# A four-layer graph network on one core: the adjacency check ahead of the last features, a table first in its queue, fp16 keys

## The chip, the core and the metric

The kernel runs on one core of a Trainium2 chip. A core has five engines with instruction queues of their own: PE (TensorE, matrix products; the load of its stationary operand is shown apart as PEld), DVE (VectorE), ACT (ScalarE), POOL (GpSimd) and SP (SyncE, which here only starts transfers). They meet through semaphores. Matrix products land in PSUM, which is handed out in banks of 128 x 512 fp32; all else lies in SBUF. Transfers from and to HBM run on 16 DMA engines, whichever engine starts them. The metric is the device time of one execution, in microseconds (us). A "granted clock" of 1.0 means that PE ran at its full clock.

## The reference, cut to what matters

x is 8 batches x 2048 nodes x 64 features; adj is a 2048 x 2048 matrix of zeros and ones with ones on its diagonal, thinner towards high node numbers; H says which of 64 hyperedges each node belongs to. Four layers follow one another, each `x = x + layer(relu(layernorm(x)))`. The change touches only work that belongs to layer 0:

```python
h = x @ W
maskEN = H.T
s = leaky_relu(h @ a_node, 0.2)
logits = where(maskEN[None, :, :] > 0, s[:, None, :], NEG)
alpha = softmax(logits, axis=-1)                  # per hyperedge, over its nodes
agg = einsum('ben,bnf->bef', alpha, h)
beta = sigmoid((h @ a_gn)[:, None, :] + (agg @ a_ge)[:, :, None])
all_he = elu(beta[..., None] * h[:, None] + (1.0 - beta[..., None]) * agg[:, :, None])
deg = maximum(adj.sum(-1), 1.0)[:, None]
industry = einsum('nm,bmf->bnf', adj / deg, x @ W_ind)
...
```

Behind these lines each node mixes its own hyperedges' `all_he` with softmax weights, and mixes the result with `industry`. Layers 1 to 3 use adj again: a graph convolution, three rounds of messages, and attention over neighbours.

## The kernel before

The kernel does not treat adj and H as dense where it need not. A node's hyperedges and near neighbours are worked through one "place" at a time, over nodes sorted by how many they have. Fixed lists in the program (`HELD`, `TIED`, `LISTED`) say for how many tiles of 128 nodes each place is made. So the kernel starts with a check that adj holds only zeros and ones and that no count exceeds those lists. The check ends in one integer, `flag`, and a branch: with 0 the short way is taken, with 1 the dense one. The branch is taken by every engine for itself, and each reads the flag first; no instruction crosses it.

Node features are kept as four tiles q, each of 128 partitions (two batches x 64 features) by 2048 nodes, worked in four chunks of 512 columns (`CW`). There are 16 tiles of 128 nodes (`NT`). The order of the instructions on each engine is not written out by hand: a scheduler sorts them by the order of the program text and by what is ready in its own estimate, within one side of the branch. What is written earlier gets the earlier turn.

**start (L594)** does three things at once. For each chunk, the layer norm: centering products (`bank<-x_ch,center`), squares, the row sums, then SQRT on ACT, RECIPROCAL on DVE (`std`, L287), the spread of the scale to all rows (`bank<-std,from_rows`), and DVE's product with it (L605). One chunk later, `features` (L649): h as h_t (features by nodes: `bank<-q,ww`, L656) and as h_n (nodes by features: `bank<-ww,q`, L662), both copied out of PSUM by ACT. And `check_adj` (L353): for each of the 16 row blocks of adj, 1 MB is loaded (L371), squared on ACT into `squares` with the row sum as `deg` (L372), and compared with its square on DVE (L373). POOL sets the diagonal to zero (L376) and starts a store to `links` (L380). PE counts the links of each pair of blocks with 13 one-column products (`seen`).

In the text, the check's matter stands behind `features` of the last chunk (L629), and its end behind the PSUM pools of the norm. That end is a row of small operations on DVE: `edges` from `seen` (L387), `count_nodes` (L422) with `classes` (L415), which makes one comparison of 128x16 for each possible count and one 128x1 comparison for each limit (L446), `crowded_lists` (L399) with 15 such comparisons (L408), joins of the maxima (L634), a transpose by PE (L636), and the flag (L639). Beside it 1/deg goes out to `rdeg` (L640 to L646).

**layer0_pairs (L782)** is the arm behind the branch. It loads `fcw` (L681), and then runs three things interleaved by a generator:

- `ranks` (L460): from the hyperedge counts of the nodes, each node's place in the sorted order, by prefix sums on DVE, with `classes` once more.
- `hyperedge_keys` (L564): for each chunk of 512 ranks and each of the 16 node tiles, a one-hot matrix `hot` (L582: is the column number equal to the node's rank?), 64 in all, and its product with H's mask (`twice`, loaded at L570).
- `aggregate` (L880): it stores h_n to `h_rows` in HBM (16 stores, L895), makes the nodes' scores (L904 to L908), loads H transposed into `cap` (L912, two transfers of 512 KB, into the slot that `squares` had), turns it into limits (L913, L914), and then for each q: `logits` (L923), their maximum (L925), the exponentials on ACT (L927), 16 transposes (L934) copied out as `et` (L182, L184), 16 products into `pa`, and some twenty small steps from `agg` to `both`.

Behind them come `by_rank` (L504, the sorted order as gather indices), the preparation of link lists, the product of adj with `x_ind` (L316), and `Pairs` (L2223), whose `fetch` gathers sorted rows of `h_rows` on POOL (L2249). SP's queue is in program order: `fcw`, the 16 stores of h_rows, HT, H, `w_ind`, then adj's blocks.

Of the kernel before, what the change touches and what calls it, by code (L numbers as in the profile page):

```python
# [19 lines left out]
P = 128  # L20
# [114 lines left out]
class Kernel:  # L135
# [76 lines left out]
    def setup(self):  # L212
# [7 lines left out]

        self.center = c.tile([P, P], F, name="center")
# [131 lines left out]
    def check_adj(self, pool, slots, seen):  # L353


        nc, adj = self.nc, self.a["adj"]
        rows = [slots.tile([P, 2, N], F, name=f"rows{i}", tag=f"q{6 + i}") for i in range(2)]
# [29 lines left out]
        nc.vector.tensor_scalar(self.edges, seen, 0.0, None, op0=OP.is_gt)  # L387
        bad = pool.tile([P, 1], F, name="bad")
        nc.vector.tensor_reduce(bad, same, axis=AX.X, op=OP.add)
        nc.vector.tensor_scalar(bad, bad, float(N * NT), None, op0=OP.is_lt)  # L390
# [5 lines left out]
        nc.vector.tensor_sub(own, deg, own)  # L396
        return bad, deg, own

    def crowded_lists(self, pool, ones, ps):  # L399

        nc = self.nc
        pn = ps.tile([P, NT, FAR], F, name="pn")
        self.mm(pn.rearrange("p t i -> p (t i)"), ones, self.edges.rearrange("p t i -> p (t i)"))
        total = pool.tile([P, NT], F, name="listed_total")
        nc.vector.tensor_reduce(total, pn, axis=AX.X, op=OP.add)
        nc.vector.memset(total[:, :1], 0.0)
        for t in range(1, NT):
            nc.vector.tensor_scalar(  # L408
                total[:, t : t + 1], total[:, t : t + 1], float(P * LISTED[t]), None, op0=OP.is_gt
            )  # L410
        bad = pool.tile([P, 1], F, name="listed_bad")
        nc.vector.tensor_reduce(bad, total, axis=AX.X, op=OP.max)
        return bad

    def classes(self, w, deg, J):  # L415

        least = w.tile([P, J + 2, NT], BF, name=f"least{J}")
        for i in range(J + 2):
            self.nc.vector.tensor_scalar(least[:, i], deg, float(J + 1 - i), None, op0=OP.is_ge)
        return least  # L420

    def count_nodes(self, pool, slots, adj_deg):  # L422

        nc = self.nc
        hm = slots.tile([P, NT, D], F, name="hm", tag="q9")
        nc.sync.dma_start(hm, self.a["H"].rearrange("(t p) e -> p t e", p=P))
        nc.vector.tensor_scalar(hm, hm, 0.0, None, op0=OP.is_gt)
        deg = self.deg
        nc.vector.tensor_reduce(deg[:, 0], hm, axis=AX.X, op=OP.add)
        nc.vector.tensor_copy(deg[:, 1], adj_deg)  # L430
        ones = pool.tile([P, P], BF, name="ones")
        nc.vector.memset(ones, 1.0)
        for which, held in enumerate((HELD + [0], TIED)):
            J = len(held) - 1
            least = self.classes(pool, deg[:, which], J)
            with self.tc.tile_pool(reuse_waits="tile", name="count_ps", bufs=1, space=PSUM) as ps:
                pn = ps.tile([P, (J + 2) * NT], F, name="pn")
                self.mm(pn, ones, least.rearrange("p k t -> p (k t)"))
                total = pool.tile([P, J + 2], F, name=f"total{which}")
                nc.vector.tensor_reduce(  # L440
                    total, pn.rearrange("p (k t) -> p k t", t=NT), axis=AX.X, op=OP.add
                )
            over = pool.tile([P, J + 2], F, name=f"over{which}")
            nc.vector.memset(over, 0.0)
            for i in range(J + 1):
                nc.vector.tensor_scalar(  # L446
                    over[:, i : i + 1], total[:, i : i + 1], float(P * held[J - i]), None,
                    op0=OP.is_gt,
                )
            if which == 0:  # L450
                nc.vector.tensor_scalar(
                    over[:, J + 1 :], total[:, J : J + 1], float(N), None, op0=OP.is_lt
                )
            bad = pool.tile([P, 1], F, name=f"crowded{which}")
            nc.vector.tensor_reduce(bad, over, axis=AX.X, op=OP.max)
            yield bad
        with self.tc.tile_pool(reuse_waits="tile", name="listed_ps", bufs=1, space=PSUM) as ps:
            yield self.crowded_lists(pool, ones, ps)
# [105 lines left out]
    def hyperedge_keys(self, w, bank, both, rank, key):  # L564
# [5 lines left out]
        nc.sync.dma_start(got, self.a["H"].rearrange("(t p) e -> p t e", p=P))  # L570
# [4 lines left out]
        line, _ = self.numbers(w, CW)  # L575
# [18 lines left out]
    def start(self, pool, slots):  # L594
# [4 lines left out]
        self.self_weight = pool.tile([P, NT], F, name="self_weight")  # L599
        with tc.tile_pool(reuse_waits="tile", name="k00", bufs=1) as k:  # L600
# [6 lines left out]
            with (  # L607
                tc.tile_pool(reuse_waits="tile", name="links_ps", bufs=1, space=PSUM) as lps,
                tc.tile_pool(reuse_waits="tile", name="ln", bufs=2) as w,
                tc.tile_pool(reuse_waits="tile", name="ln_ps", bufs=7, space=PSUM) as ps,  # L610
# [10 lines left out]
                for ch in range(NC):  # L621
# [5 lines left out]
                    if ch > 0:  # L627
                        self.features(ww, ch - 1, bank)
# [3 lines left out]
            with tc.tile_pool(reuse_waits="tile", name="check_ps", bufs=1, space=PSUM) as ps:  # L632
                for crowded in self.count_nodes(k, slots, adj_deg):
                    nc.vector.tensor_max(bad, bad, crowded)  # L634
# [245 lines left out]
    def aggregate(self, slots, raw, h_t, h_n, fcw, av, both, agg_hi, agg_lo):  # L880
        nc, tc, a = self.nc, self.tc, self.a
        with (
# [11 lines left out]
            for t in range(NT):  # L894
                nc.sync.dma_start(self.h_rows[t * P : (t + 1) * P, : NB * D], h_n(t))  # L895
# [2234 lines left out]
```

## Time and profile before

| what | us |
|---|---|
| runs, median of 3 | 2026.12 |
| runs, lowest to highest | 2022.63 to 2032.97 |
| profiled execution, whole | 1975.97 |
| profiled execution, span | 1974.2 |
| PE busy / DVE busy / POOL busy / ACT busy | 1699.7 / 1408.2 / 1035.1 / 809.4 |
| flag written (end of L639) | 106.43 |
| first gather of h_rows (L2249) | 211.20 |

The page cuts the span into 40 slices of 49 us. Busy shares are in tenths; PEclk is the granted clock in tenths; the first five slices hold all the work that the change touches:

```profile
PE   6859889999997887999999999778989899579885
...
DVE  6778778884677674877677656588989676459774
...
PEclk8868899998996888999999989889989999689887
DMA  9740223345335776233131111277788774666665
```

The 16 row blocks of adj pass in the first two slices, with the DMA engines nearly full; in the fourth slice (148 to 197 us) they stand still. A group row of the profile reads: line, engine, operation, output<-input, shapes, count, then busy us, mean ns of one, and the idle time just ahead of it with what ended most of it. In a timeline row the first number is the start, the second the time that the row covers; "x8" means eight instructions merged, and a matrix product in fp32 counts as two. Brackets hold the idle time before it. "SPq" rows are the starting of transfers, not the transfers themselves.

### The profile page before, as it was taken

Reading aid. Unit: us, or ns where it says so; the run is one execution under the profiler, and the core shown is the slowest. Engines: PE = TensorE matmul, PEld = TensorE weight load, DVE = VectorE, ACT = ScalarE, POOL = GpSimd, SP = SyncE. Lnnn points to the kernel's source line nnn. Section 1 sums busy time; section 2 is a strip of 40 time slices with the busy share of each in tenths; the row PEclk is TensorE's granted clock in tenths of the full one; section 3 lists DMA queues with packets and bytes.
Section 4 is the critical chain, followed back from the end, with each engine's and each line's share of the span. In section 5 each row is a group of like instructions: output and inputs, shape, how many; then the busy total and the mean of one; then the engine's idle time right before and its main releaser. Section 6 shows DMA issues by size and latency. Waiting matters only on the chain. (4 is left out here: it accounts for less than half of the span.)

```text
span 1974.2 us, 22337 instructions
## 1 busy us (share of the span) xinstructions
PE 1699.7 (86%) x7066; PEld 971.8 (49%) x7066; DVE 1408.2 (71%) x2389; ACT 809.4 (41%) x1627; POOL 1035.1 (52%) x959
## 2 busy tenths in 40 slices
PE   6859889999997887999999999778989899579885
PEld 2515666665324454444443444356767566345432
DVE  6778778884677674877677656588989676459774
ACT  5712344454664663222111010255666664267300
POOL 1100166766870743876765635266375641478771
PEclk8868899998996888999999989889989999689887
DMA  9740223345335776233131111277788774666665
GB/s 345 263 120 1 77 75 102 109 128 178 99 101 174 239 218 188 78 87 117 47 99 53 48 67 41 96 223 234 246 257 286 222 259 164 228 186 172 183 177 195
DMA packets 124057, 305.20 MB, mean 155 GB/s; under 512 B 29312, under 2 KB 31120, under 8 KB 118160
## 3 DMA queue, kind: packets, MB, share of 16 engines
q0 software_dynamic: 45328, 149.60, 25.2%
q1 hardware_dynamic: 76288, 149.80, 22.5%
q10 hardware_dynamic: 2304, 4.20, 0.6%
q8 instruction: 59, 0.97, 0.2%
q14 instruction: 78, 0.64, 0.1%
HBM read 240.40 MB, written 63.14 MB: 154 GB/s over the span
## 5 line engine op out<-in xcount | busy, mean ns | idle before, releaser
L2578 POOL DMA_INDIRECT raw<-sent,index x300 | 313.8, 1046 | 308.3 <-DVE part_lo L2596 156.3
L2596 DVE TENSOR_TENSOR part_lo<-raw,part_hi 128x512 fp32r<-128x512 f32 x352 | 266.2, 777 | 119.3 <-ACT part_hi L2595 108.8
L2595 ACT CAST part_hi<-raw 128x512 fp32r<-128x512 f32 x352 | 212.5, 619 | 319.0 <-PE acc L176 211.6
L1840 POOL TENSOR_TENSOR half<-half,y 128x512 f32<-128x512 f32 x192 | 247.3, 1318 | 134.0 <-DVE y L1834 128.8
L176 PE MATMUL pk<-q,w 128*128 128x512 f32 (+1 forms) x768 | 301.6, 610 | 2.4 <-DVE q L1724 0.9
L176 PE MATMUL acc<-q,ident 128*128 128x512 f32 x416 | 202.3, 613 | 22.7 <-DVE q L2909 16.5
L176 PE MATMUL acc<-part_hi,weights 128*128 128x512 f32 x365 | 177.0, 488 | 27.3 <-ACT part_hi L2595 26.7
L1834 DVE SCALAR_TENSOR_TENSOR y<-pk,bias,q 128x512 f32<-128x512 f32 x224 | 158.0, 742 | 52.1 <-PE pk L176 32.9
L176 PEld LDWEIGHTS pk<-q,w 128*128 128x128 f32 (+1 forms) x768 | 115.8, 190 | 156.0 <-issue 120.2
L176 PE MATMUL acc<-part_lo,weights 128*128 128x512 f32 x365 | 167.5, 460 | 23.3 <-DVE part_lo L2596 22.7
L2819 POOL DMA_INDIRECT ring<-f_rows,near x121 | 142.8, 1180 | 64.6 <-issue 29.6
L176 PEld LDWEIGHTS acc<-q,ident 128*128 128x128 f32 x416 | 77.1, 194 | 96.4 <-issue 43.6
L2305 POOL TENSOR_TENSOR q<-q,beta 128x512 f32<-128x512 f32 x57 | 76.1, 1337 | 72.4 <-DVE beta L2281 33.8
L176 PEld LDWEIGHTS acc<-part_hi,weights 128*128 128x128 f32 x365 | 73.7, 202 | 79.4 <-ACT part_hi L2595 45.8
L176 PEld LDWEIGHTS acc<-part_lo,weights 128*128 128x128 f32 x365 | 73.9, 202 | 73.5 <-DVE part_lo L2596 57.8
L176 PE MATMUL pp<-adj,x_ind_hi 128*128 128x512 f32 x256 | 89.3, 464 | 0.5 <-DVE q L846 0.3
L2564 ACT CAST hub_weights<-dense 128x384 fp32r<-128x384 bf16 x80 | 40.6, 511 | 102.6 <-PE acc L176 98.2
L2890 DVE TENSOR_TENSOR q<-ring,e 128x1024 f32<-128x1024 f32 x58 | 70.0, 1218 | 8.7 <-PE acc L176 8.5
L2305 POOL TENSOR_TENSOR q<-q,coef 128x512 f32<-128x512 f32 x57 | 63.1, 1108 | 20.9 <-DVE q L2328 17.6
L176 PE MATMUL pp<-adj,x_ind_lo 128*128 128x512 f32 x256 | 72.7, 403 | 0.0
L287 DVE RECIPROCAL std<-std 128x512 f32<-128x512 f32 x16 | 53.6, 3351 | 25.5 <-ACT std L286 21.6
L2489 POOL DMA_INDIRECT listed_raw<-in_adjT_dram,cell x60 | 62.2, 1037 | 16.5 <-issue 15.9
(503 smaller groups left out, 3421.6 us busy)
## 6 DMA issues: line engine op xcount, KB each, us to landing
rows<-in_adj_dram SPq DMA_DIRECT2D x16, 1024.0 KB, 9.2
adj_t<-in_adjT_dram SPq DMA_DIRECT2D x64, 256.0 KB, 3.0
own<-sent SPq DMA_DIRECT2D x52, 256.0 KB, 4.3
raw<-sent SPq DMA_DIRECT2D x52, 256.0 KB, 3.5
sent<-u SPq DMA_DIRECT2D x48, 256.0 KB, 3.7
q<-x SPq DMA_DIRECT2D x10, 1024.0 KB, 5.1
x<-q SPq DMA_DIRECT2D x9, 1024.0 KB, 4.0
links<-squares POOLq DMA_DIRECT2D x16, 512.0 KB, 8.2
```

The costliest lines, as they stand in the source:

```text
L176: self.nc.tensor.matmul(out, lhsT, rhs, start=start, stop=stop)
L287: nc.vector.reciprocal(std, std)
L1834: nc.vector.scalar_tensor_tensor(y, pks[b, half], bias[:, b : b + 1], emb[:, b], op0=OP.add, op1=OP.mult,)
L1840: add.tensor_add(acc, acc, y)
L2305: self.nc.gpsimd.tensor_tensor(x, x, by.unsqueeze(2).to_broadcast([P, NB, D]), op=OP.mult)
L2489: self.kern.behind(nc.gpsimd.indirect_dma_start(raw[:, i], None, rows, bass.IndirectOffsetOnAxis(ap=self.cell[:, c + i : c + i + 1], axis= ...
L2564: self.nc.scalar.copy(to, self.lists.dense[:, :, i * P : (i + 1) * P])
L2578: self.nc.gpsimd.indirect_dma_start(raw, None, self.rows[:], bass.IndirectOffsetOnAxis(ap=self.lists.index[:, c : c + 1], axis=0),)
L2595: nc.scalar.copy(hi, raw)
L2596: nc.vector.tensor_sub(lo, raw, hi.bitcast(F))
L2819: self.nc.gpsimd.indirect_dma_start(to, None, self.kern.f_rows[:], bass.IndirectOffsetOnAxis(ap=index, axis=0))
L2890: nc.vector.tensor_tensor(y.rearrange("n i (b f) -> n i b f", b=NB), block[:, i : i + 2, : NB * D].rearrange("n i (b f) -> n i b f", b=NB) ...
```

## The change

It has five parts.

1. Limits in tables. A constant `falling` (128x22, made by 22 one-column memsets on POOL in `setup`) holds the falling counts, so that `classes` is one DVE comparison of two broadcast operands instead of one operation for each count. `limits` puts all limits into one row, again by memsets on POOL. `count_nodes` and `count_lists` compare whole rows with it, into one tile `over` whose maximum is taken once.
2. `check_adj` holds all of the check up to the flag and 1/deg, and is called ahead of `features` of the last chunk. The hyperedges' counts are taken ahead of adj's. Its small products share one PSUM bank (`chain`) in the pool of `seen`; the norm's pool gets six banks instead of seven.
3. In `aggregate` the loads of HT and of H come first; the 16 stores of h_rows move behind the transposes of `raw`, four with each q.
4. The key's column numbers are fp16 instead of fp32.
5. The column numbers come from their own iota; the row numbers that `numbers` made along with them, and nobody read there, are gone.

```diff
 def setup(self):
+        self.falling = c.tile([P, NEAR[1] + 2], F, name="falling")
+        for i in range(NEAR[1] + 2):
+            nc.gpsimd.memset(self.falling[:, i : i + 1], float(NEAR[1] + 1 - i))
...
-    def check_adj(self, pool, slots, seen):
+    def check_adj(self, pool, slots, seen, ps, flag):
+        limit = self.limits(pool)
+        over = pool.tile([P, limit.shape[1] + 2], F, name="over")
...
-        nc.vector.tensor_scalar(self.edges, seen, 0.0, None, op0=OP.is_gt)
+        hm = slots.tile([P, NT, D], F, name="hm", tag="q9")
+        nc.sync.dma_start(hm, self.a["H"].rearrange("(t p) e -> p t e", p=P))
+        nc.vector.tensor_scalar(hm, hm, 0.0, None, op0=OP.is_gt)
+        nc.vector.tensor_reduce(self.deg[:, 0], hm, axis=AX.X, op=OP.add)
+        self.count_nodes(pool, ones, limit, over, 0, ps)
+        nc.vector.tensor_sub(self.deg[:, 1], deg, own)
+        self.count_nodes(pool, ones, limit, over, 1, ps)
...
+        nc.vector.tensor_scalar(over[:, -2:-1], bad, float(N * NT), None, op0=OP.is_lt)
+        nc.vector.tensor_scalar(self.edges, seen, 0.0, None, op0=OP.is_gt)
+        self.count_lists(pool, ones, limit, over, ps)
+        nc.vector.tensor_reduce(bad, over, axis=AX.X, op=OP.max)
+        pt = ps.tile([P, CW], F, name="chain")[:1, :P]
+        nc.tensor.transpose(pt, bad, self.ident)
+        one = pool.tile([1, 1], F, name="one")
+        nc.vector.tensor_reduce(one, pt, axis=AX.X, op=OP.max)
+        nc.vector.tensor_scalar(flag, one, 0.0, None, op0=OP.is_gt)
...
     def classes(self, w, deg, J):
         least = w.tile([P, J + 2, NT], BF, name=f"least{J}")
-        for i in range(J + 2):
-            self.nc.vector.tensor_scalar(least[:, i], deg, float(J + 1 - i), None, op0=OP.is_ge)
+        full = [P, J + 2, NT]
+        self.nc.vector.tensor_tensor(
+            least, deg.unsqueeze(1).to_broadcast(full),
+            self.falling[:, NEAR[1] - J :].unsqueeze(2).to_broadcast(full), op=OP.is_ge,
+        )
         return least
+    def limits(self, pool):
+        held = [HELD + [0], TIED]
+        values = [P * n for x in held for n in x[::-1]]
+        values += [3e9] + [P * n for n in LISTED[1:]]
+        limit = pool.tile([P, len(values)], F, name="limit")
...
+            self.nc.gpsimd.memset(limit[:, at : at + n], float(values[at]))
...
+    def count_nodes(self, pool, ones, limit, over, which, ps):
+        J = (len(HELD), NEAR[1])[which]
+        at = which * (len(HELD) + 1)
+        least = self.classes(pool, self.deg[:, which], J)
+        pn = ps.tile([P, CW], F, name="chain")[:, : (J + 2) * NT]
+        self.mm(pn, ones, least.rearrange("p k t -> p (k t)"))
+        total = pool.tile([P, J + 2], F, name=f"total{which}")
+        nc.vector.tensor_reduce(
+            total, pn.rearrange("p (k t) -> p k t", t=NT), axis=AX.X, op=OP.add
+        )
+        nc.vector.tensor_tensor(
+            over[:, at : at + J + 1], total[:, : J + 1], limit[:, at : at + J + 1], op=OP.is_gt
+        )
...
 def hyperedge_keys(self, w, bank, both, rank, key):
-        nc.sync.dma_start(got, self.a["H"].rearrange("(t p) e -> p t e", p=P))
...
-        line, _ = self.numbers(w, CW)
+        whole = w.tile([P, CW], I32, name="whole")
+        nc.gpsimd.iota(whole, pattern=[[1, CW]], base=0, channel_multiplier=0)
+        line = w.tile([P, CW], F16, name="line")
+        nc.vector.tensor_copy(line, whole)
...
 def start(self, pool, slots):
-                tc.tile_pool(reuse_waits="tile", name="ln_ps", bufs=7, space=PSUM) as ps,
+                tc.tile_pool(reuse_waits="tile", name="ln_ps", bufs=6, space=PSUM) as ps,
...
+                self.check_adj(k, slots, seen, lps, flag)
                 self.features(ww, NC - 1, bank)
-                bad, deg, adj_deg = self.check_adj(k, slots, seen)
...
 def aggregate(...):
-            for t in range(NT):
-                nc.sync.dma_start(self.h_rows[t * P : (t + 1) * P, : NB * D], h_n(t))
...
+            for s in range(2):
+                nc.sync.dma_start(cap[s * D : (s + 1) * D], a["HT"])
+            load()
             for ch in range(NC):
...
-            for s in range(2):
-                nc.sync.dma_start(cap[s * D : (s + 1) * D], a["HT"])
...
                     nc.tensor.transpose(pt[:, i], raw[:, t * P : (t + 1) * P], self.ident)
+                    nc.sync.dma_start(self.h_rows[t * P : (t + 1) * P, : NB * D], h_n(t))
```

`load` is the load of H that left `hyperedge_keys`.

## The prediction

> **What bounds the kernel now.** I read the page first, then the engines' busy time in short stretches, then the timeline and the waits of the first 212 us, since every edited line runs there. The page's chain of waits names only the tail, so it does not say what the edited stretch is worth. The stretches do. After the time, the columns are PE, PEld, DVE, ACT and POOL busy (with instruction counts), granted clock, DMA share, GB/s:
>
> ```profile
> 97.40:107.10 9.70, 1.56 (x5) 0.30 (x4) 8.20 (x92) 0.00 (x0) 0.00 (x0) 0.68 0.01 2
> 107.10:119.00 11.90, 6.17 (x34) 1.19 (x34) 10.68 (x52) 3.93 (x7) 1.90 (x6) 0.68 0.85 312
> 119.00:128.00 9.00, 2.24 (x4) 0.58 (x4) 1.84 (x6) 1.90 (x3) 0.00 (x0) 0.64 1.07 237
> 128.00:146.50 18.50, 15.20 (x37) 6.31 (x38) 16.96 (x29) 2.68 (x3) 0.32 (x2) 0.53 0.01 3
> 146.50:164.00 17.50, 17.19 (x90) 10.55 (x89) 16.63 (x41) 4.93 (x9) 0.00 (x0) 0.90 0.00 1
> ```
>
> From 97.4 to 107.1 one chain of 92 tiny DVE instructions runs and everything else stands. From 119 to 128 nearly nothing runs, while the DMA engines are full. From 128 to 164 DVE is busy for 92 and 95% of the stretches. The timeline gives the ends of those waits (start, duration, then in brackets the idle time and what ended it):
>
> ```profile
> 89.17 3.60 PE L176 MATMUL bank<-q,ww 128*128 128x512 f32 x8
> 92.60 3.73 PE L176 MATMUL bank<-ww,q 128*128 128x128 f32 x32
> 96.17 1.22 PE L176 MATMUL seen<-one_bf,squares 128*128 128x1 bf16 x43
> ...
> 97.43 0.37 DVE L387 TENSOR_SCALAR edges<-seen 128x208 bf16<-128x208 f32 x1 [6.96 <-PE seen L176]
> ...
> 106.29 0.14 DVE L639 TENSOR_SCALAR flag<-one 1x1 int32<-1x1 f32 x1
> 107.19 0.55 DVE L683 COPY av<-cols 128x128 f32<-128x128 f32 x1 [0.76 <-DVE flag L639]
> ...
> 108.39 10.17 SPq L895 DMA_DIRECT2D h_rows<-q  x16
> 118.81 1.95 SPq L912 DMA_DIRECT2D cap<-in_HT_dram  x2
> 127.98 1.23 DVE L913 TENSOR_SCALAR cap<-cap 128x2048 f32<-128x2048 f32 x1 [7.16 <-DMA cap<-in_HT_dram]
> ```
>
> PE works off 7.3 us of the last chunk's features before the 43 link counts that DVE waits for (6.96 us); then the check's chain takes 9.0 us (97.43 to 106.43); then the arm starts; its table HT is queued behind 16 stores and comes 7.16 us late.
>
> **1. The start, a small loss.** 22 one-column memsets (`falling`) now stand on POOL ahead of the memset of `ww`, and SP's first queue waits for that memset before it loads `ww` and then x. The nearest row is 15 short memsets at L2440, 0.57 us together, of 115 ns each: one starts every (0.57 - 0.115) / 14 = 0.033 us, so 22 x 0.033 = 0.7 us. At present `ww` is ready at 1.15 and its load starts at 1.26, so there is almost no slack, and the first matmul waits for x until 8.04. Take **+0.7**; bounds 0 and 22 x 0.115 = +2.5. The 25 short memsets of `limit` follow the identity on POOL, which is next needed at 19.55: hidden, about 1 us if it weren't.
>
> **2. The check.** Removed from the path: the wait behind the features. The new order on PE puts the link counts ahead of them, and the features fill PE's waits for DVE. On DVE the loops become tables; the rows of 97 to 108 (busy us, mean ns):
>
> ```profile
> L446 DVE TENSOR_SCALAR over<-total 128x1 f32<-128x1 f32 x34 | 2.5, 136 | 0.0
> L419 DVE TENSOR_SCALAR least<-deg 128x16 bf16<-128x16 f32 x22 | 1.9, 163 | 0.0
> L408 DVE TENSOR_SCALAR listed_total<-listed_total 128x1 f32<-128x1 f32 x15 | 1.1, 143 | 0.0
> ```
>
> These 5.5 us become one 128x352 comparison, priced by the 128x208 TENSOR_TENSOR rows (366 ns at L488) at about 0.55, and two of 0.15. There is one maximum instead of three, with no joins.
>
> A wait is added: the first count (`total<-chain`, 128x14) stands on DVE ahead of the last chunk's RECIPROCAL, now at 74.76, and waits for a matmul that stands on PE behind 46 link counts. These start at 73.93 and come every 0.03, so it ends near 75.5, and the 0.38 reduction makes the RECIPROCAL start near 75.9: **+1.1**. Behind it are the scale factors, PE's products with them, and DVE's last two comparisons, so I count it whole (bounds 0 to +1.5). Three small operations between the last comparisons add 0.4.
>
> So the last comparison ends not at 90.06 but at 90.06 + 0.7 + 1.1 + 0.4 = 92.3. Then: last link count 93.0 (one feature product of 0.9 stands before it); product 0.9 and the 128x352 count to 94.4; reduction 0.53, edges' count and reduction to 95.9; limits and maximum to 96.2; one product and a quarter of a tile on PE, transpose, maximum, flag near 97.5; the transpose and copy of `rows`, which stand before the branch on DVE, to 98.4. With the 0.76 of the branch DVE starts the arm at 99.1, and SP with it (its store of `rdeg` waits for that copy, between its reading of the flag and its branch). PE still has 12 x 0.23 = 2.8 us of features, reaches the branch at 100.9 and the arm's first matmul near 101.6; DVE would want it at 99.1 + 1.9 - 0.55 = 100.5, so PE is late next. That matmul was at 109.06. **Net -7.5**, the two losses of 1 and 2 included; bounds -6 (the features hold it) and -9.5 (losses 0, features hidden). PSUM: six banks for seven; of the nine banks that a norm takes, the one reused sixth was read long before, so 0, up to +1.
>
> **3. HT first.** SP issues `fcw` (1.11), HT (1.95), H (0.58) and only then the 16 stores. HT's issue ends 3.1 us into the arm; its 1 MB, with nothing ahead, takes as long as the x loads of 1 MB (5 to 8 us by their rows), so it is there about 9 us in at worst. DVE asks at 99.1 + 9 (the work now from 107.2 to 116.7, less the shorter `least`): no wait left. **-7.2**, bounds -5 and -7.2. H is wanted five us later still. HT's load waits for the last `links` stores out of the same slot: issued at 90.7, 8.2 us to land, so 99 to 101, about when SP gets there. The stores of h_rows move behind; first reader is the gather at 211.20, 100 us later: hidden. The gathers and the mask on POOL change places with some memsets: under 1 us, beside matmuls.
>
> **4. The rank's `least`** in the arm: 13 of 0.073 spacing (0.95) become one of about 0.4: **-0.55**. One 0.15 cast falls away too.
>
> **5. One-hot keys from fp16.** The 64 keys, and the nearest 16-bit row:
>
> ```profile
> L582 DVE TENSOR_SCALAR hot<-linef,rank_here 128x512 bf16<-128x512 f32 x64 | 28.0, 479 | 3.2 <-PE bank L176 3.0
> L2437 DVE TENSOR_SCALAR q<-q,ownf 128x780 bf16<-128x780 bf16 x1 | 0.4, 421 | 0.0
> ```
>
> Keys start 0.395 us apart (six in 2.46 us). The 780-column 16-bit row, 421 ns, is shorter than the 512-column fp32 one: fp32 costs 0.49 ns a column (1227 ns at 2048 less 479 at 512), so 16-bit near half of that, 0.25. 512 x 0.245 = 0.13 us each, 64 x 0.13 = 8.3 us of DVE. How much reaches the end? [...] The trace: granted clock 0.53 at 128 to 146.5 and 0.90, 0.75, 0.92 in the three stretches to 206.5; the same bf16 products come every 0.43 us in the first and every 0.22 when warm; DVE waits on PE for 11 us already (`aggs` 5.6, `hot` 3.0, `et` 2.3). [...] a product at 0.43 is slower than a key at 0.27, PE paces the stage, and the fp16 part gives 0: the total would be -15.2. By the rows the clock does return, and up to 8.3 comes through: -23.6. Between them I take half, by the rows, since two of three stretches were at 0.9: **-4.3**.
>
> **Sum**: -7.5 - 7.2 - 0.55 - 4.3 = **-19.5**. The profiled execution took 1974.2 in its span and 1.8 around it: 1976.0 becomes 1956.5. The median of the runs is 2026.1, 50 us above that execution, with a spread of 10; nothing in the trace tells why. I take off the same microseconds (in proportion it would be 20.0): **2006.6**.
>
> **Rivals.** About 0.5% (10 us) is what can be told from no change.
> A, as above, about 2006 (2001 to 2013): 0.55.
> B, DVE sets the pace throughout: all 8.3 come through[...]: -24 to -30, about 2000: 0.20. For it: DVE 92 to 95% busy at 128 to 164; against: PE busy at 20.5 of 20.5 at 164 to 184.
> C, PE paces the arm and the features hold the branch: -6 - 7.2 - 0.5 = -13.7, about 2012: 0.13.
> D, it doesn't do what it says: HT still comes late behind the `links` stores (say 5 of 7.2 lost) and the check ends behind the features (-4): about 2020: 0.08. Against: 2 GB/s in the stretch before the arm.
> E, slower: granted clock. PE is busy 1541 us after 212 us, at 0.911 on the mean, with slices between 0.6 and 0.9. If the earlier start shifts the later bursts so that the mean falls by 1.3%, to 0.899, 20 us are gone; from 0.893 (30 us) it is slower by 0.5%, about 2037. For it: clock differs among stretches of like work; against: those later stages have the same instructions and waits. 0.04.
> The range 1991 to 2018 leaves out the ends of A and B, most of D, and E, under 0.2 together. Faster 0.83, same 0.13 (D and the edges of A and C), slower 0.04.
>
> **What would show it.** First matmul near 8.7; RECIPROCAL of the last chunk near 76.5; flag near 97.5, arm near 99 to 101; no wait for HT; keys at about 0.35 us of duration; the gather of h_rows near 191.5 instead of 211.2; after that, the same distances between stages. Wrong it would be if that gather comes 20 us earlier and the end doesn't, if a key still takes 0.48, or if the flag comes after 103.

## The result, and the profile after

| | before | after |
|---|---|---|
| median, us | 2026.76 (2022.63 to 2032.97, 4 runs) | 2001.78 (1985.33 to 2011.05, 4 runs) |
| ratio | | 0.9876, 95% interval 0.9835 to 0.9917 |
| the same two on another chip (that of e5 to e8), median, us | 2025.42 (14 runs) | 1998.68 (6 runs) |
| ratio there | | 0.9854, 95% interval 0.9813 to 0.9896 |
| profiled execution, span, us | 1974.2 | 1983.5 |

The kernel is 25 us faster (16.8 to 33.4 by the interval), where 19.5 were forecast. The two profiled spans show the opposite sign: the profile of before lies 50 us below that kernel's own other runs, the one of after only 16. The spans are therefore no measure of the change. On the chip of e9 to e12 below, 44 runs of the kernel before took 1970.24 to 1986.89, median 1979.06, 46 us less than on that of e5 to e8: the level goes with the chip, and the profile of before, 1975.97, fits the faster one. On which chip it was taken is not on record. The stretch that the change touches is a better measure, and it is compared up to the first gather of h_rows.

The timeline of the changed kernel, with the rows that answer to those shown of before (start, duration, in brackets the idle time and what ended it):

```profile
75.70 0.69 ACT L290 ACTIVATE std<-bank,eps 128x512 f32<-128x512 f32 x1 [0.65 <-PE bank L176]
77.08 0.39 DVE L461 TENSOR_REDUCE total<-chain 128x14 f32<-128x224 f32 x1 [2.53 <-PE chain L176]
77.39 3.34 DVE L291 RECIPROCAL std<-std 128x512 f32<-128x512 f32 x1
...
91.37 1.19 PE L176 MATMUL seen<-one_bf,squares 128*128 128x1 bf16 x42
93.60 0.38 DVE L405 TENSOR_SCALAR edges<-seen 128x208 bf16<-128x208 f32 x1 [0.40 <-PE seen L176]
97.22 0.14 DVE L412 TENSOR_SCALAR flag<-one 1x1 int32<-1x1 f32 x1
97.49 2.84 PE L176 MATMUL bank<-ww,q 128*128 128x128 f32 x24
98.42 0.25 DVE L692 COPY av<-cols 128x128 f32<-128x128 f32 x1 [0.46 <-DVE rows L424]
...
100.32 1.10 SPq L917 DMA_DIRECT2D cap<-in_HT_dram  x2
102.16 15.36 SPq L1003 DMA_DIRECT2D h_rows<-q  x16
107.82 1.23 DVE L930 TENSOR_SCALAR cap<-cap 128x2048 f32<-128x2048 f32 x1 [1.31 <-DMA cap<-in_HT_dram]
184.78 0.58 DVE L962 TENSOR_SCALAR aggs<-pa,den 64x64 f32<-64x64 f32 x2 [2.58 <-PE pa L176]
185.61 0.38 SPq L1009 DMA_DIRECT2D h_rows<-hb  x1
189.49 1.02 POOL L2267 DMA_INDIRECT q<-h_rows,order  x1 [1.24 <-DMA h_rows<-hb]
```

And of the kernel before, the rows of these events that were not shown yet:

```profile
74.04 0.69 ACT L286 ACTIVATE std<-bank,eps 128x512 f32<-128x512 f32 x1 [0.65 <-PE bank L176]
74.76 3.35 DVE L287 RECIPROCAL std<-std 128x512 f32<-128x512 f32 x1 [0.84 <-ACT std L286]
...
206.32 0.58 DVE L945 TENSOR_SCALAR aggs<-pa,den 64x64 f32<-64x64 f32 x2 [2.59 <-PE pa L176]
207.15 0.37 SPq L991 DMA_DIRECT2D h_rows<-hb  x1
211.20 1.02 POOL L2249 DMA_INDIRECT q<-h_rows,order  x1 [77.77 <-DVE upto L544]
```

The wait for the link counts fell from 6.96 to 0.40 us; the check's chain runs from 93.60 to 97.36 instead of 97.43 to 106.43, and TensorE works on features beside it. HT's loads start 18.5 us earlier, and the wait for them fell from 7.16 to 1.31. A new wait, 2.53, stands ahead of the RECIPROCAL. The gather comes at 189.49 instead of 211.20.

What the gather waits for is not the sorted order, which is ready some 30 us earlier, but the last write into h_rows, the store of `hb`. That is made of `raw`, the nodes' scores, which in before are complete at 120.3 us, but by its turn in the program it stands right behind the last `aggs`; no run wrote it earlier. In all 14 profiles of this case that store starts 3.9 to 4.6 us ahead of the gather, whatever engine its row names as the releaser. So the arm up to the gather is as long as the chain from HT over `logits` and `et` to `aggs` takes; the keys come into it through the turns that they take on VectorE.

The stretches of the changed kernel (after the time: PE, PEld, DVE, ACT, POOL busy with counts, granted clock, DMA share, GB/s):

```profile
93.60:98.42 4.82, 4.82 (x27) 3.11 (x27) 2.99 (x14) 2.89 (x5) 0.87 (x2) 1.00 0.27 109
98.42:107.82 9.40, 5.71 (x38) 2.39 (x36) 7.36 (x31) 4.13 (x7) 1.48 (x5) 0.91 0.73 149
107.82:121.50 13.68, 12.28 (x29) 3.41 (x29) 10.55 (x16) 3.55 (x5) 0.32 (x2) 0.62 1.00 329
121.50:139.00 17.50, 17.33 (x81) 9.72 (x80) 16.16 (x41) 3.96 (x6) 0.00 (x0) 0.85 0.01 1
139.00:156.00 17.00, 16.08 (x100) 10.61 (x100) 14.05 (x48) 4.46 (x9) 0.00 (x0) 0.90 0.00 0
156.00:173.00 17.00, 17.00 (x91) 10.73 (x90) 13.82 (x39) 4.94 (x9) 0.00 (x0) 0.90 0.00 1
```

There is no longer a stretch in which TensorE stands (before, it was busy for 1.56 of 9.70 us and for 2.24 of 9.00). The low clock lasts one stretch of 13.7 us; before, the granted clock was 0.53 to 0.68 from 97 to 146.5. And the groups of VectorE in the arm (busy us, mean ns, then idle time and its releaser):

```profile
L606 DVE TENSOR_SCALAR hot<-line,rank_here 128x512 bf16<-128x512 f16 x64 | 19.7, 348 | 1.2 <-PE bank L176 0.3
...
L184 DVE COPY et<-pt 128x512 f32<-128x512 f32 x8 | 5.5, 688 | 3.4 <-PE pt L951 3.3
...
L962 DVE TENSOR_SCALAR aggs<-pa,den 64x64 f32<-64x64 f32 x8 | 2.3, 283 | 5.3 <-PE pa L176 5.3
```

A key takes 348 ns instead of 479, 131 ns less where 130 were taken: 64 x 0.131 = 8.4 us in all. But VectorE still waits for TensorE at `et` and `aggs`, 3.3 and 5.3 us (2.3 and 5.6 before), so not all of that need reach the end.

### The profile page after: what moved, and what is told of

Its sections match the earlier page's. It is cut to its first block, busy times and chain, and to the rows that moved or that the text cites. A ratio compares the mean times of both kernels' runs of the same rounds, so it can differ in the third digit from the quotient of the medians.

```text
span 1983.5 us, 22268 instructions
## 1 busy us (share of the span) xinstructions
PE 1699.7 (86%) x7066; PEld 973.2 (49%) x7066; DVE 1392.2 (70%) x2266; ACT 809.3 (41%) x1627; POOL 1037.4 (52%) x1005
## 5 line engine op out<-in xcount | busy, mean ns | idle before, releaser
L176 PE MATMUL acc<-q,ident 128*128 128x512 f32 x416 | 208.6, 627 | 39.1 <-issue 27.1
L2837 POOL DMA_INDIRECT ring<-f_rows,near x121 | 138.8, 1147 | 70.1 <-issue 31.7
L176 PE MATMUL pp<-adj,x_ind_lo 128*128 128x512 f32 x256 | 72.3, 402 | 0.0
```

Source lines behind the costliest of these rows:

```text
L176: self.nc.tensor.matmul(out, lhsT, rhs, start=start, stop=stop)
L2837: self.nc.gpsimd.indirect_dma_start(to, None, self.kern.f_rows[:], bass.IndirectOffsetOnAxis(ap=index, axis=0))
```

## Experiments

Each profile is cut at the same events: S, the start of the last chunk's square root on ScalarE (`std`); the flag; `av`, VectorE's first copy in the arm; G, the first gather of h_rows; the end. In us:

| kernel | S | S to flag | flag to av | av to G | G | G to end |
|---|---|---|---|---|---|---|
| before | 74.0 | 32.3 | 0.9 | 104.0 | 211.2 | 1763.0 |
| e8, before again | 74.3 | 32.1 | 0.9 | 108.7 | 216.0 | 1807.3 |
| e12, before, a third profile | 72.3 | 31.8 | 0.9 | 103.6 | 208.7 | 1761.5 |
| after | 75.7 | 21.5 | 1.2 | 91.1 | 189.5 | 1794.0 |
| e5, after again | 73.5 | 21.3 | 1.2 | 90.1 | 186.2 | 1810.3 |
| e1, e11: after, fp32 keys | 75.8, 74.7 | 21.5, 21.5 | 1.2, 1.2 | 96.7, 95.2 | 195.2, 192.6 | 1762.7, 1755.9 |
| e2: after, stores first | 75.1 | 21.5 | 1.2 | 101.3 | 199.1 | 1755.8 |
| e3: after, features first | 75.9 | 26.6 | 1.1 | 92.5 | 196.0 | 1756.4 |
| e4: after, without tables | 73.8 | 24.8 | 1.1 | 89.7 | 189.4 | 1768.0 |
| e6: after, both losses moved | 75.3 | 21.5 | 1.2 | 90.5 | 188.5 | 1805.1 |
| e7: after, delayed | 73.5 | 23.6 | 13.5 | 90.0 | 200.6 | 1803.2 |
| e9: before, fp16 keys alone | 74.6 | 31.2 | 0.9 | 105.1 | 211.8 | 1760.9 |
| e10: before, HT first alone | 73.1 | 31.2 | 0.9 | 97.0 | 202.2 | 1769.9 |

e1 to e4 ran on one chip, e5 to e8 on a second, e9 to e12 on a third; the profiles of before and after were taken apart from these. So most distances below compare one profile with one of another chip; where two are of the same chip, it is said. The columns separate what a single time mixes. S wanders by 3.6 us, though x is issued at 2.5 or 3.15 in all of them and little else differs up to there. S to flag repeats within 0.2 in six profiles of the changed check. G to end goes with the chip, not with the kernel: 1756 to 1768 in e1 to e4, 1803 to 1810 in e5 to e8, 1756 to 1770 in e9 to e12.

Of e1 to e4 there is one time each, of before one on their chip: 1959.7, 1956.6, 1954.2 and 1959.1 against 1980.1. They are not in the order of G, and single runs of one kernel differ by more (1986.5 to 2010.2 in e5), so these four are read at G alone.

**One part undone in the changed kernel (e1 to e4).**

Fp32 keys:

```diff
-        line = w.tile([P, CW], F16, name="line")
+        line = w.tile([P, CW], F, name="line")
```

> The changed kernel with the keys' column numbers in fp32 again; all else stays. Read at the first gather of h_rows, which closes the edited stretch (189.5 us in the changed kernel, 211.2 before). If about half of the keys' saving reaches the end of the stretch (the forecast's step 5): 193 to 195. If DVE sets the pace alone, all 8.3 us come back: near 198. If PE sets the pace: below 190.5. The key's duration goes from 348 back to 479 ns in each case, and the arm still starts at 98.4.

A key took 480 ns, and G came at 195.2: 5.7 later than in the first profile of after. In the arm alone it is 96.7 less 90.1 or 91.1, so 5.6 to 6.6 of the 8.4 that the keys differ by: a little over the half (193 to 195), well under the whole (198).

The 16 stores back ahead of HT and H:

```diff
+            for t in range(NT):
+                nc.sync.dma_start(self.h_rows[t * P : (t + 1) * P, : NB * D], h_n(t))
             for s in range(2):
                 nc.sync.dma_start(cap[s * D : (s + 1) * D], a["HT"])
             load()
...
-                    nc.sync.dma_start(self.h_rows[t * P : (t + 1) * P, : NB * D], h_n(t))
```

> The changed kernel with the 16 stores of h_rows ahead of the loads of HT and H again. If the queue position made the old wait: HT is asked for 10 us later, lands about 20.8 us into the arm as before (near 119), DVE waits 5 to 10 us for it instead of 1.3, and the first gather moves from 189.5 to 195 to 198. If the wait is only exchanged for DVE's other work (the keys need H, which is late too) it is at the upper end of that; if something else bounds the stretch (PE at low clock), the gather stays within 2 us of 189.5.

G came at 199.1, 1 us beyond the upper end of what was expected, and the arm took 101.3, which is 10.2 to 11.2 more. The timeline of this kernel has the old wait back:

```profile
99.45 10.59 SPq L917 DMA_DIRECT2D h_rows<-q  x16
110.28 1.13 SPq L919 DMA_DIRECT2D cap<-in_HT_dram  x2
118.75 1.23 DVE L932 TENSOR_SCALAR cap<-cap 128x2048 f32<-128x2048 f32 x1 [7.44 <-DMA cap<-in_HT_dram]
```

The wait is 7.44 against 1.31, a difference of 6.1; the arm lost 10 to 11. So some 4 us more hang on it. Its stretches show where (columns as above):

```profile
109.80:118.80 9.00, 2.23 (x4) 0.48 (x4) 1.56 (x9) 1.87 (x2) 0.00 (x0) 0.59 1.10 254
118.80:137.20 18.40, 15.10 (x34) 5.59 (x35) 16.42 (x30) 3.27 (x4) 0.36 (x2) 0.55 0.05 9
```

For 18.4 us behind the wait the granted clock is 0.55, and 34 products take 15.1 us of TensorE; in the changed kernel the 17.5 us from 121.5 have 81 products at 0.85. The counts are not of the same work: 53 of the 81 are products and transposes of 128x128, against 10 of the 34. Like ones can be set side by side in the kernel before, which has the same wait and 0.53 behind it (128 to 146.5 us), and in the changed one: a key's product (`bank<-hot,twice`) takes 630 ns on the mean in that stretch of before and 509 in those 17.5 us; one of `pl<-cap,from_rows` takes 1096 there, and in the changed kernel 1008 in the stretch at 0.62 and 686 behind it. Over the whole arm the granted clock is 0.85 here, 0.86 in after and 0.88 in e5. By (1 - clock) x length that is 15.2 us lost against 12.8 and 10.8: an estimate of 2 to 4 us for the clock's share, from these three numbers.

The last chunk's features ahead of the check in TensorE's queue:

```diff
-                self.check_adj(k, slots, seen, lps, flag)
                 self.features(ww, NC - 1, bank)
+                self.check_adj(k, slots, seen, lps, flag)
```

> The changed kernel with the features of the last chunk ahead of the check in the text again; the tables stay. If the order is what matters: the link counts wait for 7.3 us of feature products, edges come near 100 instead of 93.6, the flag near 103.5 instead of 97.2, the arm on DVE near 105, and the gather at 194 to 196. If PE's late arrival at the branch (its first product of the arm at 100.2, though DVE was there at 98.4) had already taken the order's gain, the gather moves by less than 3 us.

G 196.0. S to flag is 26.6, 5.1 more, and the arm 1.4 to 2.4 more. The timeline shows the wait for the link counts again:

```profile
94.91 3.73 PE L176 MATMUL bank<-ww,q 128*128 128x128 f32 x32
...
98.48 1.22 PE L176 MATMUL seen<-one_bf,squares 128*128 128x1 bf16 x43
99.74 0.38 DVE L405 TENSOR_SCALAR edges<-seen 128x208 bf16<-128x208 f32 x1 [5.96 <-PE seen L176]
102.48 0.14 DVE L412 TENSOR_SCALAR flag<-one 1x1 int32<-1x1 f32 x1
```

From `edges` to the flag it is even shorter here, 2.7 us instead of 3.6, with no features left beside it. So the new order costs that chain 0.9 and saves all but 0.4 of the wait of 6.

The comparisons one by one instead of by tables, those with the limits too, and without the 22 memsets:

```diff
-        self.nc.vector.tensor_tensor(
-            least, deg.unsqueeze(1).to_broadcast(full),
-            self.falling[:, NEAR[1] - J :].unsqueeze(2).to_broadcast(full), op=OP.is_ge,
-        )
+        for i in range(J + 2):
+            self.nc.vector.tensor_scalar(least[:, i], deg, float(J + 1 - i), None, op0=OP.is_ge)
```

> The changed kernel with the single comparisons in loops again instead of the tables (no falling and limit rows, so x is asked for 0.65 us earlier); the check stays ahead of the features. If the tables carry their own share: 2 to 5 us more of small DVE operations between the last comparison and the flag, flag at 99 to 102, gather at 191 to 194. If the features on PE, which end near 100, cover that chain anyway: the gather stays within 1.5 us of 189.5 although the flag is later.

S to flag 24.8, 3.3 more than with tables; but S was 1.9 earlier than in after, flag to av and av to G a little shorter, and G came at 189.4. Measured from S to G, the tables are worth 1.8 (115.6 against 113.8) or 2.9 (against e5's 112.7); at G itself nothing was seen, because the start wandered by as much. The flag, at 98.6, came earlier than the 99 to 102 of the first expectation.

**The whole again, its two losses, and a delay (e5 to e8).** The profile of after had taken 1794 us from G to the end, against 1763 before. Whether the change gave something back there was the question.

> The changed kernel once more, unchanged. Open: after the gather of h_rows its first profile took 1794 us to the end, the kernel before took 1763, and four kernels with parts undone took 1756 to 1768. Theory V (the execution, not the change): here the stretch from that gather to the end is again within 1750 to 1770, the gather is near 189.5, and the time is 20 to 27 us below the kernel before. Theory G (the earlier start meets a worse pattern of gathers or clock in layers 2 and 3 and gives it back): the stretch is again above 1785, and the time is within 10 us of the kernel before.

> The kernel before, unchanged, for a profile on the same chip as e5 to e7. Gather of h_rows at 211; from there to the end Theory V says 1750 to 1770, the same as in e5 within some 10 us, and as in e6 and e7. Theory G says clearly shorter than in e5.

Neither theory had the numbers right: on this chip both kernels take 1807 to 1810 from G on. The comparison still decides for V, since the difference between the kernels is 3 us, not 30. G came at 186.2 against 216.0, 29.8 earlier, and the medians differ by 26.7. Of the 29.8, the check gave 10.8, the arm 18.6 and S 0.8, less 0.3 from flag to av. The arm of before was slow in e8: its granted clock was 0.76 from 146.5 to 164, where the first profile had 0.90.

```diff
-        for i in range(NEAR[1] + 2):
-            nc.gpsimd.memset(self.falling[:, i : i + 1], float(NEAR[1] + 1 - i))
...
-        nc.vector.reciprocal(std, std)
+        self.recip = nc.vector.reciprocal(std, std).ins
...
+        with self.tc.issue_after(self.recip):
+            nc.vector.tensor_reduce(
```

(The memsets are now made at the head of `check_adj`.)

> All of the change is kept; the 22 memsets of falling go behind the memset of ww on GpSimd (into the check), and the first count's reduction is ordered behind the last chunk's RECIPROCAL on VectorE. Theory (both losses are real and on the path): x is issued at 2.50 instead of 3.15, the last chunk's RECIPROCAL starts at 74.8 to 75.6 instead of 77.4, the flag at 94.4 to 95.2 instead of 97.2. Then either the check stays ahead of TensorE's features (gather of h_rows 2 to 2.7 us earlier, 186.8 to 187.5), or these features hold TensorE and only about the start's 0.65 comes through (gather near 188.8). The time is 0.7 to 3 us below e5, which is at the edge of what five rounds can tell. Rival (losses hidden anyway): gather unchanged at 189.5.

Two rows of the timeline, with the new place of the count:

```profile
75.28 0.69 ACT L288 ACTIVATE std<-bank,eps 128x512 f32<-128x512 f32 x1 [0.65 <-PE bank L176]
76.00 3.35 DVE L289 RECIPROCAL std<-std 128x512 f32<-128x512 f32 x1 [1.87 <-ACT std L288]
...
86.19 0.39 DVE L462 TENSOR_REDUCE total<-chain 128x14 f32<-128x224 f32 x1
...
95.22 0.38 DVE L477 TENSOR_REDUCE listed_total<-chain 128x16 f32<-128x208 f32 x1 [0.84 <-PE chain L176]
```

The RECIPROCAL starts 0.72 after S, as in before; with the count ahead it is 1.69 in after, so the added wait is **0.97**. Yet S to flag is 21.5 with and without it. What is gained ahead of the last comparison is lost behind it: the lists' count waits 0.84 for TensorE instead of 0.21, and the count for 128x22 comes 2.33 instead of 2.05 (e5) behind the last comparison. The start loss can't be seen at S either: x is issued at 2.51, first product at 8.04, and S is at 75.28, later than e5's 73.54 with x at 3.15. From the first product to S took 64.2 to 67.2 us in all these profiles, at granted clocks that differ (0.74 from 60 to 70 us in after, 0.90 in e5). Its median of 1997.86 is not to be told from e5's 1998.68. It is no better kernel.

```diff
+        for _ in range(26):
+            nc.vector.tensor_scalar(hm, hm, 1.0, None, op0=OP.mult)
         nc.vector.tensor_reduce(bad, over, axis=AX.X, op=OP.max)
```

> The changed kernel with 26 more multiplications by one over 128x1024 fp32 on VectorE ahead of the check's last reduction, some 0.73 us each (0.479 for 512 columns and 0.49 ns for each more), 19 us in all: about what the change brought. Theory S (a shift of the arm is carried unchanged to the end): the gather of h_rows comes near 208.3, the time is 17 to 20 us above e5. Theory G (the time depends on where the later bursts fall, not on the shift): the time is anywhere within 10 us of e5 or more than 25 above it. Nothing is left out of the computation.

The scheduler put 12 of the 26 among the check's operations, where they partly fill waits, and 14 in a row behind the flag (10.13 us). Hence `av` came 14.5 later than in e5 and not 19; G came 14.4 later. The ratio to the kernel before is 0.9921 (0.9890 to 0.9953) against 0.9854, a difference of 0.0067, or 13.6 us; by the medians it is 10.5, just above the 10 of Theory G. A shift at the arm's start thus goes through to G whole, and to the end as nearly as the runs can tell.

**One part alone (e9 to e12).** The part is put into the kernel before.

```diff
-        line, _ = self.numbers(w, CW)
+        whole = w.tile([P, CW], I32, name="whole")
+        nc.gpsimd.iota(whole, pattern=[[1, CW]], base=0, channel_multiplier=0)
+        line = w.tile([P, CW], F16, name="line")
+        nc.vector.tensor_copy(line, whole)
```

> The kernel before with one part of the change alone: the one-hot keys from fp16. The distance from the arm's first VectorE copy (av) to the gather of h_rows was 104.0 and 108.6 in two profiles of the kernel before, 91.1 and 90.1 in two of the changed one, and 96.7 with the change but fp32 keys. Theory P (the keys are on the path whatever comes before them): 98 to 102.5, some 6 us less than before, and the time 4 to 8 us below. Theory T (TensorE, colder behind the late table, sets the pace here; the keys pay only together with the early table): above 103, time unchanged.

> The kernel before once more, for its own spread on this chip: distance from av to the gather between 103 and 109, from the last chunk's standard deviation (ScalarE) to the flag 32.3, from the gather to the end as in the three runs beside it within 10 us.

The distance from av to G is 105.1: nothing gained at the gather against 103.6 on the same chip. The groups of VectorE with keys alone, and then those of the kernel before on that chip:

```profile
L585 DVE TENSOR_SCALAR hot<-line,rank_here 128x512 bf16<-128x512 f16 x64 | 20.2, 348 | 3.8 <-PE bank L176 2.8
...
L184 DVE COPY et<-pt 128x512 f32<-128x512 f32 x8 | 5.5, 688 | 6.1 <-PE pt L937 6.1
...
L948 DVE TENSOR_SCALAR aggs<-pa,den 64x64 f32<-64x64 f32 x8 | 2.3, 283 | 6.2 <-PE pa L176 6.2
```

```profile
L582 DVE TENSOR_SCALAR hot<-linef,rank_here 128x512 bf16<-128x512 f32 x64 | 28.0, 480 | 3.2 <-PE bank L176 3.1
...
L184 DVE COPY et<-pt 128x512 f32<-128x512 f32 x8 | 5.5, 692 | 2.1 <-PE pt L934 2.0
...
L945 DVE TENSOR_SCALAR aggs<-pa,den 64x64 f32<-64x64 f32 x8 | 2.3, 284 | 5.7 <-PE pa L176 5.6
```

VectorE is busy 7.8 us less with the keys, and waits 4.0 us more for TensorE at `et` alone. That is theory T in so far as TensorE sets the pace. The 22 timed runs speak differently: ratio 0.9977 (0.9962 to 0.9992), 4.7 us faster, 1.6 to 7.5 by the interval. The clock does not settle it: 0.74 was granted from 164 to 184 here, but 0.74, 0.76 and 0.74 in the three profiles of the kernel before, and 0.77 over the arm, where e12 has 0.76. How much the keys alone are worth in most executions stays open between the two.

```diff
+            for s in range(2):
+                nc.sync.dma_start(cap[s * D : (s + 1) * D], a["HT"])
             for t in range(NT):
                 nc.sync.dma_start(self.h_rows[t * P : (t + 1) * P, : NB * D], h_n(t))
...
-            for s in range(2):
-                nc.sync.dma_start(cap[s * D : (s + 1) * D], a["HT"])
```

> The kernel before with HT's two loads ahead of the 16 stores of h_rows alone. With the change but the stores first, the distance from av to the gather was 101.3 against 90.1 and 91.1: 10 to 11 us, more than the 7.2 of the wait itself. Theory 1 (the wait and a colder TensorE behind it): distance 94 to 98.5, 10 us less than before; the granted clock in the 20 us behind the table above 0.8 instead of 0.53. Theory 2 (the wait alone): 97 to 101.5, some 7 us less. The time falls by as much.

97.0 from av to G: 6.6 less than e12 on the same chip, 7.0 and 11.6 less than the other two profiles of before. The wait for HT is gone; the row of e12 and then that of this kernel:

```profile
125.74 1.23 DVE L913 TENSOR_SCALAR cap<-cap 128x2048 f32<-128x2048 f32 x1 [7.27 <-DMA cap<-in_HT_dram]
```

```profile
114.31 1.22 DVE L913 TENSOR_SCALAR cap<-cap 128x2048 f32<-128x2048 f32 x1
```

Two stretches of it, and then those of e12:

```profile
119.00:128.00 9.00, 6.92 (x10) 2.23 (x9) 7.30 (x14) 1.82 (x2) 0.00 (x0) 0.52 0.90 270
128.00:146.50 18.50, 18.45 (x81) 11.08 (x82) 13.03 (x33) 4.29 (x8) 0.32 (x2) 0.77 0.01 1
```

```profile
119.00:128.00 9.00, 0.18 (x1) 0.00 (x0) 2.22 (x2) 0.21 (x1) 0.00 (x0) 0.50 0.92 175
128.00:146.50 18.50, 17.10 (x56) 8.56 (x58) 16.97 (x33) 3.27 (x4) 0.32 (x2) 0.60 0.00 0
```

With the table in time TensorE works in the first stretch, and does 81 products (not all the same) in the second instead of 56. But 97.0 lies in the ranges of both theories, the clock of 0.77 misses the "above 0.8" of Theory 1, and the gain of 6.6 is no more than the wait of 7.27 that fell away. Over the arm the clock rose from 0.76 to 0.82, by the estimate above worth another 7.4, which did not come through. A reason that fits, but that no run took apart: the arm still holds 80.8 us of work of VectorE in its 97.0 (82.5 of 103.6 in e12, 74.2 of 91.1 in after). The end moved by less than the arm: ratio 0.9984 (0.9969 to 0.9998), 2.8 us (0.4 to 6.1). Its G to end is 8 us longer than in e9 and e12. Why was not found.

> The changed kernel with fp32 keys a second time, now timed. The distance from av to the gather is again near 96.7, 6 us above the changed kernel's 90 to 91, and the time 4 to 8 us above the changed kernel's ratio of 0.9854 to the kernel before, at 0.988 to 0.990. If the keys cost only their half (4.3) the distance is below 95.

95.2 from av to G, between the two theories. The ratio is 0.9928 (0.9901 to 0.9955), nearer to 1 than the 0.988 to 0.990 expected: a gain of 14.3 us without the fp16 keys. Against the 26.7 of e5 that would leave 12 to the keys, twice what the arm shows; but the changed kernel itself was not timed on this chip, so this difference is of two chips.

The gain at G and that of the times can be compared where a chip has both (G against that chip's profile of before, times by the medians): e5 29.8 and 26.7, e6 27.6 and 27.6, e7 15.5 and 16.3, e10 6.4 and 2.8, e11 16.1 and 14.4, e9 a loss of 3.1 and a gain of 4.7. So apart from e9 the end moves as the gather does, within 4 us.

## Why the prediction was right, by its steps

The forecast of -19.5 came true in sign, in the main of its mechanism and, within the runs' spread, in size: 25.0 (16.8 to 33.4) in the first runs; on the chip of e5 to e8 it was 26.7 (21.1 to 37.9 by the interval), a little more than forecast. At the gather it was 191.5 forecast, and 189.5 and 186.2 measured. Layers after it kept their distances, as e5, e6, e7 and e8 show on one chip (1803 to 1810). Rival E, the clock downstream, has nothing for it: from G to the end the granted clock is 0.92 in e5 and in e8, and the 0.915 and 0.904 of their whole executions differ by what lies ahead of G. (The 0.911 that the prediction set at the work after 212 us is the mean of the whole execution too; there it is 0.92.) Rival D falls with the wait for HT, C with a gather that came sooner than its 13.7 allow. Rival B is not told from A by the time: 2001.78 lies at the near end of A's 2001 to 2013, and 25.0 and 26.7 both lie in B's 24 to 30. For it speaks that TensorE was granted more (0.86 and 0.88 over the arm instead of 0.73 to 0.76); against it stand e1 and e11, where less than all of the keys' 8.4 comes back, and VectorE's waits for TensorE of 3.3 and 5.3 that are left.

1. *The start.* x was issued 0.65 later (0.7 taken). That it reaches the end was not shown: the first stage varies by 3 us for itself.
2. *The check.* The added wait was 0.97 (1.1 taken), and e6 shows that it is worth nothing when removed. The last comparison and the flag came 0.6 and 1.3 sooner behind S than the sum had them: 17.0 where 92.3 less the forecast S of 74.74 makes 17.6, and 21.5 where 97.5 less it makes 22.8. The 128x352 comparison took 512 ns (0.55 taken). The arm's first product came 24.5 behind S instead of 35.0 before, so the features did not hold TensorE beyond what was allowed. By e3 and e4, 5.1 of the 10.7 from S to the flag are the order, 3.3 the tables; the rest was not taken apart.
3. *HT first.* "No wait left" was wrong by 1.31. As a term for this part alone the 7.2 was good: e10 gained 6.6 on its chip. Together with fp16 keys it was too small, because it held the wait alone: there the late table costs 10 to 11 us (e2). The 4 us above the 6.1 of the wait go with the stretch behind it, where the granted clock is 0.55 for 18.4 us with the wait, and 0.62 for 13.7 and then 0.85 without; the estimate of 2 to 4 us fits, but no run changed the clock alone. The clock had been weighed for the keys. It should have been weighed here too, together with what VectorE then allows.
4. *The rank's `least`.* e4 puts the 13 comparisons of the arm back too, and its arm of 89.7 is no longer than 90.1 and 91.1. So the 0.55 was not seen at G.
5. *Keys.* With the table early, 4.1 to 6.6 of 8.3 come through (e1 and e11 against after and e5); half, 4.3, lies in that. The half was a middle between two readings and followed from neither, so that it fits is in part luck. The reading that gave nothing took the 0.43 us per product of the stretch at 0.53 for the whole stage; that TensorE would stay so slow was the author's estimate, and in before the three stretches behind it were granted 0.90, 0.74 and 0.92. With the table late, the profile of e9 has none at the gather. So by the profiles a TensorE that paces the stage fits the kernel before, and the rows fit the changed one: the two ends of this step were two kernels. The timed runs of e9 leave room for a part in between.

The excess over the forecast at the gather, 2 us in one pair of profiles and 10 in the other, is made of 1.3 in the check, 0.4 from flag to av, and 1.3 or 7.0 in the arm (91.1 or 90.1 against 104.0 or 108.7; forecast 11.6 less, the 92.4 from 99.1 to 191.5 against 104.0), with S on both sides of it. The arm of the kernel before is what varies, 103.6 to 108.7 in three profiles; that of the changed kernel stays within 89.7 to 92.5 in the six that have its order and its keys (after and e3 to e7). So the 29.8 at the gather between e8 and e5 holds a slow arm of before; whether the timed runs of before had it there too, one profile does not show.

## What to carry to other kernels

A wait's length is not yet the gain of removing it. Here 6.1 us of wait cost 10 to 11 when put back into the changed kernel, and 7.3 gave 6.6 when taken out of the old one. Where TensorE stands during a wait, look at the granted clock and at the time of like products in the next 20 us (in before 0.53, and 630 ns for a key's product against 509 at 0.85 in the changed kernel), and at how full the other engine's time is (80.8 of 97.0 us in e10), before you price it. An operation made cheaper on one engine need not be worth its own saving, and what it is worth can hang on another part of the same change: the keys, 8.4 us less on VectorE, gave 4.1 to 6.6 at the gather with the table early and nothing there with it late. Test parts alone and undone, since the two need not agree. Where a single profile of a kernel wanders by tens of microseconds (spans of 1970.2 to 2023.3 for before), cut both traces at the same events and compare the distances; and take both on one chip.

## What the runs showed of the hardware that was not expected

From the first gather of h_rows to the end, the same kernel (before) took 1763.0, 1807.3 and 1761.5 us in three profiles, the last two on different chips, at mean granted clocks of 0.911, 0.904 and 0.913 over the whole and of 0.92 in each from the gather on. The timed runs say the same: a median of 2025.42 over 14 runs on one chip, of 1979.06 over 44 on another. All four profiles of one chip lay within 1803 to 1810, whatever the kernel. The first profile of the changed kernel, at 1794, had run at 0.917, as high as any. So the clock does not explain it. As far as the chip is on record it goes with the chip; what differs there stays open.

The first stage, from the first product to S, took 64.2 to 67.2 us with nearly the same instructions, and its granted clock differed between profiles in the same ten microseconds (0.74 and 0.90). That is more than the losses of 0.65 and 0.97 that were looked for in it.
